# First group's tokens loaded first, normalized and turned ahead of the branch, and the folded output weights made in parts, in a three-stage attention and MLP kernel

## The chip, the cores and the metric

The kernel runs on one core of one Trainium2 chip. The metric is the device time of one execution in microseconds (us). The engines are named as in the profile: PE multiplies matrices, DVE, ACT and POOL work element by element, SP issues transfers (DMA). Each engine takes its instructions in order; between engines they wait on semaphores.

## The reference

The input `x` is (2, 256, 128, 128) in float32: B, T, FB and C. Three residual steps follow each other:

```python
cm = _causal_mask(x.shape[1])
bm = _band_mask(x.shape[2], BAND)                       # BAND = 16
xt = _ln(x, ln_t_w, ln_t_b).transpose(0, 2, 1, 3)
x = x + _mha(xt, t_wi, t_bi, t_wo, t_bo, H_T, cm).transpose(0, 2, 1, 3)
xf = _ln(x, ln_f_w, ln_f_b)
x = x + _mha(xf, f_wi, f_bi, f_wo, f_bo, H_F, bm)
xn = _ln(x, ln_n_w, ln_n_b)
h = jax.nn.gelu(xn @ w1.T + b1, approximate=False)
x = x + (h @ w2.T + b2)
```

`_ln` is a layer norm over C. `_mha` is attention with 4 heads of 32: three projections, scores with a mask, softmax, weighted sum, output projection. The first runs over T for each band with a causal mask, the second over the bands for each time with a band mask. The MLP is 128 to 512 to 128.

## The kernel before

**Two paths.** `load_constants` issues the loads of the weights (on ACT's queue) and of `cols`, `rows` and the first tokens `x0` (on SP's queue). `fold` (L341) multiplies the norm's scale into the projection weights (`wf`, `bq`) and bounds the scores from the weights: products `gk`, `gq`, `tests`, `tp`, then `ok`, `allok` and an integer `flag` on DVE. Every engine reads `flag` and branches (`tc.If`, L1161). With bounded scores `bounded_path` runs, in which softmax needs no maximum; this is the path of these inputs. The other one, `shifted_path`, is not executed.

**Groups.** The bounded path works on groups of 512 tokens (`NT` = 4 tiles of 128). A group is `OverTime` (attention over T), `OverBands` or `FeedForward`; there are 128 of each. A group's steps are methods:

- `statistics`: mean and variance on DVE (BATCH_NORM_STATS2, BATCH_NORM_AGGREGATE: `stats`, `mv`)
- `root_by_scalar`, `refine`: the inverse root by ln and exp on ACT (`lnv`, `root`), then three small operations on DVE (`vy`, `vy`, `rstd`)
- `normalize`: four operations on DVE that write `xh` with 33 elements to a row of 32
- `turn`: a transposition by 32x32 blocks on DVE (`z`) and four stores of `z` to a DRAM tile `turned`
- `fetch`: one load of `turned` as `xnT`, with the channels on the partitions
- `queries_keys`, `values`: the projections `qp`, `kp`, `vp` on PE, copied by ACT to `qT`, `kT`, `v`
- `time_scores`: the products `sp` of the new group's first half and the old group's second half, then exponentials `p` on ACT, masks and sums on POOL
- `weigh`, `invert`, `divide`, `output`, `finish`: `rp`, `op`, reciprocals, `u`, `oT`, `yp`, and the residual sum

**What `normalize` reads.** It takes its input through `longer`, which gives a slice of 160 elements, 32 more than a tile has:

```python
def longer(quad, i, a):
    return quad.rearrange("p s t c -> p (s t c)")[:, i * P - a : (i + 1) * P + D - a]
```

`a` is 0 for the first three tiles and 32 for the last. `x0` has the shape (P, NT, NT, C), and group g takes `x0[:, :, g]`.

**The order.** `run` (L1029) writes the order out by hand: for n from -12 on, it calls each step of the groups around n, and `InOrder` keeps each engine's instructions in that order. Normalizing group n+4 and fetching n+3 go ahead of the projections of n+2 and the scores of n and n+1. PSUM has 8 banks; `time_scores` takes them by name, and `bank` otherwise by turns. A tile that takes over a bank waits for the last reader of the one before.

**The folded rest.** At n = -4 `fold_rest` (L989) makes, for each attention, `bp` (a product of the value weights and the norm's shift), `bv`, the negated output weights `wn`, and `orow` (on ACT, multiplied by the output weights on PE as `op`, and summed with `rows` on DVE), then `b1p`, `b1` and `w1f` for the MLP. `warm` (L1022) follows with eight products of 384 columns whose result nobody reads.

Of the kernel before, what the change touches and what calls it, by code (L numbers as in the profile page):

```python
# [10 lines left out]
F32 = mybir.dt.float32  # L11
# [8 lines left out]
P = 128  # L20
# [3 lines left out]
EPS = 1e-5  # L24
# [14 lines left out]
def load_constants(ctx, tc, x, t_wiT, t_woT, f_wiT, f_woT, w1T, w2T, cols, rows):  # L39
    nc = tc.nc  # L40
    B, T, FB, C = x.shape
    k = Consts()
    k.NI = w1T.shape[1] // P
    const = ctx.enter_context(tc.tile_pool(name="const", bufs=1))
    k.const = const
    k.cols = const.tile([P, 16], F32, name="cols_sb")
    nc.sync.dma_start(k.cols, cols)
    k.rows = const.tile([P, 3, C], F32, name="rows_sb")
    for i in range(3):
        nc.sync.dma_start(k.rows[:, i, :], rows[i : i + 1, :].partition_broadcast(P).squeeze(1))  # L50


    k.x0 = const.tile([P, NT, NT, C], F32, name="x0")
    for i in range(NT):
        f = i // (T // P) * NT
        nc.sync.dma_start(k.x0[rows_of(i)], BoundedPath.of_times(x[0], i, slice(f, f + NT)))

    def weight(src, n, name):
        t = const.tile([P, n], F32, name=name)
        nc.scalar.dma_start(t, src)  # L60
        return t

    k.wiT = (weight(t_wiT, 3 * C, "t_wiT_sb"), weight(f_wiT, 3 * C, "f_wiT_sb"))
    k.woT = (weight(t_woT, C, "t_woT_sb"), weight(f_woT, C, "f_woT_sb"))
    k.w1T = weight(w1T, k.NI * P, "w1T_sb")
    k.w2T = const.tile([P, k.NI, C], F32, name="w2T_sb")
    nc.scalar.dma_start(k.w2T, w2T.rearrange("(j p) c -> p j c", p=P))
    k.ident = const.tile([P, P], F32, name="ident")
    make_identity(nc, k.ident)
    k.mhalf = const.tile([P, NT], F32, name="mhalf")  # L70
    nc.vector.memset(k.mhalf, -0.5)
    dram = ctx.enter_context(tc.tile_pool(name="dram", bufs=1, space=DRAM))
    k.x1 = [dram.tile([T, FB, C], F32, name=f"x1_{b}") for b in range(B)]
    return k
# [263 lines left out]
                    nc.sync.dma_start(outv[:, t0 + g : t0 + g + NT, :], res)  # L338


def fold(tc, k):  # L341

    nc = tc.nc
    const = k.const
    C = P
    scale = 1.0 / math.sqrt(D)
    tensor, vector, scalar = InOrder(tc, nc.tensor), InOrder(tc, nc.vector), InOrder(tc, nc.scalar)

    def col(i):
        return k.cols[:, i : i + 1]

    k.ones = const.tile([P, P], F32, name="ones")
    nc.vector.memset(k.ones, 1.0)
    k.wf, k.bq = [], []
    tests = const.tile([P, 6], F32, name="tests")
    with tc.tile_pool(name="foldp", bufs=2) as fp, tc.tile_pool(name="foldps", bufs=1, space=PSUM) as pp:
        scalar.preload_act_table_set(EXP_SET)

        bp = pp.tile([P, 2], F32, name="bp")
        for a in range(2):
            tensor.matmul(bp[:, a : a + 1], k.wiT[a][:, 0:C], col(5 * a + 1), start=True, stop=True)
        for a in range(2):
            c0 = 5 * a
            wf = const.tile([P, 3 * C], F32, name=f"wf{a}")
            vector.tensor_scalar(wf[:, 0:C], k.wiT[a][:, 0:C], col(c0), scale, ALU.mult, ALU.mult)
            vector.tensor_scalar(wf[:, C : 3 * C], k.wiT[a][:, C : 3 * C], col(c0), None, ALU.mult)
            bq = const.tile([P, 1], F32, name=f"bq{a}")
            vector.tensor_scalar(bq, bp[:, a : a + 1], col(c0 + 2), scale, ALU.add, ALU.mult)  # L370
            k.wf.append(wf)
            k.bq.append(bq)
        brs = []
        for a in range(2):
            brp = pp.tile([1, P], F32, name=f"brp{a}")
            tensor.matmul(brp, k.bq[a], k.ident, start=True, stop=True)
            br = fp.tile([1, P], F32, name="br")
            scalar.copy(br, brp)
            brs.append(br)

        for a in range(2):
            wf, wo = k.wf[a], k.woT[a]
            br = brs[a]
            gk = pp.tile([P, P], F32, name="gk", tag=f"gk{a}")
            tensor.matmul(gk, wf[:, C : 2 * C], wf[:, C : 2 * C], start=True, stop=True)
            gq = pp.tile([P, P], F32, name="gq", tag=f"gq{a}")
            tensor.matmul(gq, wf[:, 0:C], wf[:, 0:C], start=True, stop=False)
            tensor.matmul(gq, br, br, start=False, stop=True)
            gs = fp.tile([P, P], F32, name="gs")
            scalar.copy(gs, gk)  # L390
            vector.tensor_tensor(gs, gq, gs, ALU.mult)
            for h in range(H):
                r = rows_of(h)
                vector.tensor_reduce(tests[r, 3 * a : 3 * a + 1], gs[r, r], AX.X, ALU.add)
            for j, w in ((1, wf[:, 2 * C : 3 * C]), (2, wo)):
                sq = fp.tile([P, P], F32, name="sq")
                scalar.activation(sq, w, AF.Square, accum_out=tests[:, 3 * a + j : 3 * a + j + 1])
        tp = pp.tile([P, 6], F32, name="tp")
        tensor.matmul(tp, k.ones, tests, start=True, stop=True)
        ok = fp.tile([P, 6], F32, name="ok")  # L400
        for a in range(2):
            vector.tensor_scalar(
                ok[:, 3 * a : 3 * a + 1], tp[:, 3 * a : 3 * a + 1], SAFE * SAFE / (C * (C + 1)), None, ALU.is_le
            )
            vector.tensor_scalar(
                ok[:, 3 * a + 1 : 3 * a + 3], tp[:, 3 * a + 1 : 3 * a + 3], LARGE, None, ALU.is_le
            )
        allok = fp.tile([P, 1], F32, name="allok")
        vector.tensor_reduce(allok, ok, AX.X, ALU.min)
        flag = const.tile([P, 1], I32, name="flag")  # L410
        vector.tensor_copy(flag, allok)
    return nc.values_load(flag[0:1, 0:1], min_val=0, max_val=1)


# [10 lines left out]
class Group:  # L425
# [10 lines left out]
    def load(self):  # L436

        if self.before is not None:
            self.before()

    def bias(self):
        pass
# [196 lines left out]
def rows_of(h):  # L639
    return slice(h * D, (h + 1) * D)  # L640
# [223 lines left out]
class BoundedPath:  # L864
# [121 lines left out]
                for g, part, _, store in run:  # L986
                    yield FeedForward(self, partial(part, "x2", g), partial(part, "res", g), None, partial(store, g))

    def fold_rest(self):  # L989

        k, tensor, vector, scalar = self.k, self.tensor, self.vector, self.scalar
        C = P
# [1 line left out]
        def col(i):  # L994
            return k.cols[:, i : i + 1]

        k.wn, k.orow = [], []
        for a in range(2):
            c0 = 5 * a

            bp = self.bank([P, 1], "bp")
            tensor.matmul(bp, k.wiT[a][:, 2 * C : 3 * C], col(c0 + 1), start=True, stop=True)
            bv = self.small.tile([P, 1], F32, name="bv")
            scalar.activation(bv, bp, AF.Identity, bias=col(c0 + 4))
            wn = self.once.tile([P, C], F32, name=f"wn{a}")
            scalar.mul(wn, k.woT[a], -1.0)
            k.wn.append(wn)
            orow = self.once.tile([P, C], F32, name=f"orow{a}")
            scalar.activation(orow, k.ones, AF.Copy, scale=bv)
            op = self.bank([P, C], "op")  # L1010
            tensor.matmul(op, orow, k.woT[a], start=True, stop=True)
            vector.tensor_tensor(orow, op, k.rows[:, a, :], ALU.add)
            k.orow.append(orow)
        b1p = self.bank([P, k.NI], "b1p")
        for j in range(k.NI):
            tensor.matmul(b1p[:, j : j + 1], k.w1T[:, j * P : (j + 1) * P], col(11), start=True, stop=True)
# [2 lines left out]
        k.w1f = self.once.tile([P, k.NI * P], F32, name="w1f")  # L1019
        scalar.activation(k.w1f, k.w1T, AF.Copy, scale=col(10))  # L1020

    def warm(self):  # L1022


        for _ in range(8):
            bank = self.bank([P, 3 * P], "warm")
            self.tensor.matmul(bank, self.k.ones, self.k.wf[0], start=True, stop=True)

    def run(self, x, out):  # L1029
        groups = list(self.groups(x, out))  # L1030

        def do(n, *names):
            if 0 <= n < len(groups):
# [6 lines left out]
        def do_at(n, kind, *names):  # L1040
            if at(n, kind):
                do(n, *names)
# [4 lines left out]
        due = {n: [i for i in run0 if run0[0] + due[i] == n] for n in range(-12, len(groups) + 2)}  # L1047
        A = RUN // NT

        self.scalar.preload_act_table_set(EXP_SET)  # L1050
        for n in range(-12, len(groups) + 2):
            feeds = [at(n - 2 + i, FeedForward) for i in range(5)]
            bands = [at(n - 2 + i, OverBands) for i in range(5)]
# [36 lines left out]
            if n < 0:  # L1090
                do(n + 5, "statistics")
            do_at(n + 5, FeedForward, "statistics")
            if n == -4:
                self.fold_rest()
                self.warm()
            do(n - 1, "weigh")
            do(n - 1, "invert_exactly" if turn else "invert")
            if new is not None:
# [17 lines left out]
                    do_at(n + A, OverBands, "statistics", "root")  # L1116
            do_at(n + 2, OverTime, "queries_keys", "take_query", "take_key")
            do_at(n + 1, OverBands, "queries_keys", "take_query", "take_key")
            do_at(n + 5, OverTime, "root_by_scalar", "refine")
            for i in due[n]:  # L1120
                do(i, "root_by_scalar", "refine")
            do_at(n, OverTime, "bias")
# [1 line left out]
                do(n - 2, "output", "finish")  # L1124
            do_at(n + 2, OverTime, "values", "take_values")
            do_at(n + 1, OverBands, "values", "take_values")
            if old is not None or new is not None:

                b = self.banks
# [11 lines left out]
def conv_seq_kernel(  # L1141
# [15 lines left out]


    k = load_constants(ctx, tc, x, t_wiT, t_woT, f_wiT, f_woT, w1T, w2T, cols, rows)
    bounded = fold(tc, k)  # L1160
    with tc.If(bounded > 0) as cmp:  # L1161
        bounded_path(tc, k, x, out)
    with cmp.Else():
# [38 lines left out]
```

## Time and profile before

| what | value |
|---|---|
| time, median of 4 runs | 2710.82 us (2707.32 to 2711.22) |
| the profiled execution's own time | 2710.08 us |
| its span | 2708.4 us |
| mean granted clock of PE | 0.998 |
| busy: PE, DVE, ACT, POOL | 99%, 84%, 68%, 69% |
| `flag` written, first statistics | 12.84 us, 13.94 us |
| first `qp` | 27.39 us |

A row of the timeline has the start in us, the busy time in us, the engine, the line (L859 is the recording helper of all steps), the operation, output<-input, shapes and the count; in brackets the idle time before it and what ended it. SPq rows are transfers being issued, PEld rows are weight loads of PE. A row of busy time by stretches has the stretch, its length, then PE, PEld, DVE, ACT and POOL with the number of instructions, the granted clock, the DMA share and GB/s.

### The profile page before, as it was taken

How to read it: one execution, taken by the hardware profiler on the slowest of the kernel's cores; microseconds unless marked ns; L12 is line 12 of the kernel's file. 1: busy time of each engine (PE TensorE's matmuls, PEld its weight loads, DVE VectorE, ACT ScalarE, POOL GpSimd, SP SyncE). 2: the span in 40 equal slices, each digit the busy share in tenths (PEclk: the TensorE clock that was granted, in tenths of full speed). 3: DMA queues.
4: the chain of work that ended last, by engine and by line, in shares of the span. 5: the costliest groups of instructions: out<-in, count | busy, mean ns of one | idle time of the engine just before them, and what ended most of it. 6: DMA issues, size and time to landing. Idle time of an engine off the chain costs nothing.

```text
span 2708.4 us, 139654 instructions
## 1 busy us (share of the span) xinstructions
PE 2677.2 (99%) x60470; PEld 1832.1 (68%) x60470; DVE 2278.9 (84%) x6708; ACT 1845.0 (68%) x3620; POOL 1864.3 (69%) x2169
## 2 busy tenths in 40 slices
PE   8999999999999999999999999999999999999998
PEld 5676767666766666666667766666666666666665
DVE  7999999999999987868769779688697796886874
ACT  6888888888888874655745646557456465565563
POOL 4887888788878876667657666666676666665762
PEclk9999999999999999999999999999999999999999
DMA  6555555555555535445444444454444444544533
GB/s 155 140 150 143 149 150 142 148 151 143 149 144 148 143 100 131 108 120 133 109 124 125 111 127 115 118 130 114 121 126 110 124 119 118 130 110 123 134 92 84
DMA packets 471442, 346.00 MB, mean 128 GB/s; under 512 B 43296, under 2 KB 405152, under 8 KB 470816
## 3 DMA queue, kind: packets, MB, share of 16 engines
q1 hardware_dynamic: 469568, 335.92, 48.3%
q8 instruction: 476, 7.80, 1.3%
q14 instruction: 150, 1.23, 0.2%
q10 hardware_dynamic: 1248, 1.05, 0.2%
HBM read 169.03 MB, written 167.77 MB: 124 GB/s over the span
## 4 chain that ended last, share of the span: by engine, by line
PE 82%; DVE 14%; DMA 2%; issue 1%; ACT 0%; SPq 0%; DVEq 0%; ACTq 0%
PE zp L859 17%; PE hp L859 14%; PE sp L859 10%; PE op L859 8%; PE rp L859 7%; PE vp L859 7%; PE qp L859 6%; PE kp L859 6%; PE yp L859 6%; DVE xh L859 3%; DVE stats L859 2%; DVE z L859 2%; DVE u L859 2%; DVE rp L859 2%; DVE sp L859 1%; DVE x L859 1%
## 5 line engine op out<-in xcount | busy, mean ns | idle before, releaser
L859 ACT ACTIVATE hT<-hp,b 128x512 f32<-128x512 f32 x512 | 346.7, 687 | 533.1 <-PE hp L859 518.1
L859 POOL TENSOR_SCALAR_AFFINE_SELECT pf<-pf 128x512 f32<-128x512 f32 x768 | 477.0, 635 | 265.6 <-ACT pf L859 239.2
L859 DVE TENSOR_SCALAR xh<-x,mv,rstd 128x160 f32<-128x160 f32 x1536 | 596.7, 430 | 14.2
L859 PEld LDWEIGHTS zp<-w2T_sb,hT 128*32 128x32 f32 x16384 | 459.3, 110 | 61.5 <-issue 37.2
L859 PE MATMUL zp<-w2T_sb,hT 128*32 128x128 f32 x16384 | 475.7, 273 | 0.2 <-ACT hT L859 0.2
L859 PE MATMUL hp<-xnT,w1f 128*32 128x512 f32 x4096 | 474.6, 592 | 0.0
L859 ACT ACTIVATE p<-sp 128x512 f32<-128x512 f32 (+1 forms) x1024 | 417.1, 501 | 15.9 <-PE sp L859 4.2
L859 POOL TENSOR_SCALAR_AFFINE_SELECT p<-p 128x1024 f32<-128x1024 f32 x256 | 280.0, 1094 | 188.8 <-ACT p L859 188.8
L859 PE MATMUL sp<-qT,kT 32*128 32x128 f32 (+1 forms) x8192 | 361.4, 310 | 3.2 <-DVE oT L859 1.8
L859 PEld LDWEIGHTS sp<-qT,kT 32*128 32x128 f32 x8192 | 309.4, 185 | 56.8 <-ACT kT L859 47.9
L859 PEld LDWEIGHTS vp<-wf,xnT 128*32 128x32 f32 x8192 | 232.8, 110 | 157.2 <-issue 138.8
L859 POOL TENSOR_TENSOR p<-p,p 128x512 f32<-128x512 f32 x256 | 328.7, 1284 | 10.7
L859 DVE BATCH_NORM_STATS2 stats<-x 128x6 f32<-128x128 f32 x1536 | 326.9, 275 | 0.1
L859 ACT ACTIVATE pf<-sp 128x512 f32<-128x512 f32 x512 | 264.7, 603 | 60.4 <-PE sp L859 59.6
L859 PEld LDWEIGHTS hp<-xnT,w1f 128*32 128x32 f32 x4096 | 156.3, 110 | 189.9 <-issue 115.5
L859 DVE STREAM_TRANSPOSE z<-xh 128x512 f32<-128x512 f32 x384 | 273.2, 712 | 13.2
L859 DVE TENSOR_TENSOR res<-zp,res 128x512 f32<-128x512 f32 x128 | 87.4, 683 | 223.7 <-PE zp L859 223.2
L859 PE MATMUL yp<-wn,oT 128*32 128x128 f32 x8192 | 272.1, 273 | 0.0
L859 PE MATMUL vp<-wf,xnT 128*32 128x128 f32 x8192 | 270.9, 273 | 0.0
L859 POOL TENSOR_TENSOR rstd<-rstd,mhalf 128x4 f32<-128x4 f32 x248 | 256.6, 1035 | 20.7
L859 PE MATMUL qp<-xnT,wf 128*32 128x512 f32 x2048 | 267.3, 592 | 2.0 <-ACT p L859 2.0
L859 ACT ACTIVATE qT<-qp,bq 128x512 f32<-128x512 f32 x256 | 176.0, 688 | 134.4 <-PE qp L859 134.2
(92 smaller groups left out, 4001.6 us busy)
## 6 DMA issues: line engine op xcount, KB each, us to landing
turned<-z SPq DMA_DIRECT2D x1536, 64.0 KB, 2.3
xnT<-turned SPq DMA_DIRECT2D x384, 256.0 KB, 3.1
x<-in_x SPq DMA_DIRECT2D x128, 256.0 KB, 4.2
x<-res SPq DMA_DIRECT2D x256, 128.0 KB, 2.4
x<-x SPq DMA_DIRECT2D x128, 256.0 KB, 4.3
out<-res SPq DMA_DIRECT2D x256, 128.0 KB, 2.5
w1T_sb<-in_w1T ACTq DMA_DIRECT2D x1, 256.0 KB, 6.0
w2T_sb<-in_w2T ACTq DMA_DIRECT2D x1, 256.0 KB, 7.6
```

The costliest lines, as they stand in the source:

```text
L859: return self.tc.keep_in_program_order(emit(*args, **kwargs))
```

## The change

The first tokens are loaded in two portions: token 0 of each block of `x0` in four loads of 64 KB, then `rows`, then the remaining three tokens in four loads of 192 KB. Group 0's `statistics`, `root_by_scalar`, `refine`, `normalize`, `turn` and `fetch` and group 1's `statistics`, `root_by_scalar` and `refine` are issued inside `fold`, ahead of the branch, in tiles of their own; in the bounded path these steps are emptied by `follow`. `warm` becomes twelve products of 128 columns inside `fold`, behind `tp`. `fold_rest` is made in three parts: part 0 behind `values` of group 0, part 1 behind those of group 1, part 2 behind those of group 2. For n < 0, `root_by_scalar` and `refine` of group n+5 come behind `values`. The second load of the activation table is gone.

```diff
+    def tokens(a, n):
+        for i in range(NT):
+            f = i // (T // P) * NT + a
+            nc.sync.dma_start(k.x0[rows_of(i), :, a : a + n], BoundedPath.of_times(x[0], i, slice(f, f + n)))
+
+    tokens(0, 1)
     k.rows = const.tile([P, 3, C], F32, name="rows_sb")
     for i in range(3):
         nc.sync.dma_start(k.rows[:, i, :], rows[i : i + 1, :].partition_broadcast(P).squeeze(1))
-    for i in range(NT):
-        f = i // (T // P) * NT
-        nc.sync.dma_start(k.x0[rows_of(i)], BoundedPath.of_times(x[0], i, slice(f, f + NT)))
+    tokens(1, NT - 1)
...
+class Ahead:
+    def __init__(self, ctx, tc, k):
+        self.tc, self.k = tc, k
+        self.vector, self.scalar, self.sync = InOrder(tc, tc.nc.vector), InOrder(tc, tc.nc.scalar), InOrder(tc, tc.nc.sync)
+        self.pool = ctx.enter_context(tc.tile_pool(name="ahead", bufs=1))
+        self.work = self.small = self
+        self.dram = ctx.enter_context(tc.tile_pool(name="aheadd", bufs=1, space=DRAM))
...
+    def group(self, g):
+        def src(i=None, a=0):
+            return self.k.x0[:, :, g] if i is None else BoundedPath.longer(self.k.x0, i * NT + g, a)
+
+        return OverTime(self, src, None)
...
-def fold(tc, k):
+def fold(ctx, tc, k):
...
+    ahead = Ahead(ctx, tc, k)
+    k.first = g0, g1 = ahead.group(0), ahead.group(1)
...
             k.bq.append(bq)
+        g0.statistics()
+        g0.root_by_scalar()
+        g0.refine()
         brs = []
...
             brs.append(br)
+        g0.normalize()
+        g0.turn()
...
         tensor.matmul(tp, k.ones, tests, start=True, stop=True)
+
+        warm = pp.tile([P, P], F32, name="warm", tag="gk0")
+        for _ in range(12):
+            tensor.matmul(warm, k.ones, k.wf[0][:, 0:C], start=True, stop=True)
+        g1.statistics()
+        g1.root_by_scalar()
+        g0.fetch()
         ok = fp.tile([P, 6], F32, name="ok")
...
         vector.tensor_copy(flag, allok)
+        g1.refine()
     return nc.values_load(flag[0:1, 0:1], min_val=0, max_val=1)
...
+    def follow(self, ahead):
+        done = ["statistics", "root_by_scalar", "refine"]
+        self.mv, self.rstd = ahead.mv, ahead.rstd
+        if hasattr(ahead, "xnT"):
+            self.xnT = ahead.xnT
+            done += ["normalize", "turn", "fetch"]
+        for name in done:
+            setattr(self, name, lambda: None)
...
-    def fold_rest(self):
+    def fold_rest(self, part):
...
-        k.wn, k.orow = [], []
-        for a in range(2):
+        if part == 0:
+            k.wn, k.orow = [], []
+        if part < 2:
+            a = part
...
             k.orow.append(orow)
+            return
         b1p = self.bank([P, k.NI], "b1p")
...
-    def warm(self):
-        for _ in range(8):
-            bank = self.bank([P, 3 * P], "warm")
-            self.tensor.matmul(bank, self.k.ones, self.k.wf[0], start=True, stop=True)
-
     def run(self, x, out):
         groups = list(self.groups(x, out))
+        for g, ahead in zip(groups, self.k.first):
+            g.follow(ahead)
...
-        self.scalar.preload_act_table_set(EXP_SET)
         for n in range(-12, len(groups) + 2):
...
             if n < 0:
                 do(n + 5, "statistics")
             do_at(n + 5, FeedForward, "statistics")
-            if n == -4:
-                self.fold_rest()
-                self.warm()
...
-            do_at(n + 5, OverTime, "root_by_scalar", "refine")
+            if n >= 0:
+                do_at(n + 5, OverTime, "root_by_scalar", "refine")
...
             do_at(n + 2, OverTime, "values", "take_values")
             do_at(n + 1, OverBands, "values", "take_values")
+            if n < 0:
+                if n >= -2:
+                    self.fold_rest(n + 2)
+                do(n + 5, "root_by_scalar", "refine")
+            if n == 0:
+                self.fold_rest(2)
```

## The prediction

> **What bounds the kernel now.** I read the page first, then busy time by stretches, the timeline of the first 60 us and the DMA answers there.
>
> ```profile
> span 2708.4 us, 139654 instructions
> PE 2677.2 (99%) x60470; PEld 1832.1 (68%) x60470; DVE 2278.9 (84%) x6708; ACT 1845.0 (68%) x3620; POOL 1864.3 (69%) x2169
> ```
> ```profile
> 27.40:48.86 21.46, 18.26 (x333) 10.73 (x332) 17.69 (x61) 18.54 (x44) 11.59 (x11) 1.00 0.55 151
> 48.86:2650.00 2601.14, 2591.28 (x58864) 1773.79 (x58868) 2226.04 (x6526) 1800.35 (x3524) 1840.11 (x2141) 1.00 0.50 128
> ```
>
> PE is the bound from 48.86 us on (2591.28 of 2601.14 busy; a round of the first branch takes 7.30 us and PE is busy for all of it). Behind that point the built program of the changed kernel has the same instructions in the same order on each engine. So the change is worth what it moves the moment at which PE stops waiting, and that moment lies in these rows of the timeline:
>
> ```profile
> 3.34 3.39 SPq L56 DMA_DIRECT2D x<-in_x  x4
> 13.78 0.06 DVE L881 MEMSET eps<- 128x1 f32 x1 [0.79 <-DVE flag L859]
> 18.73 1.78 SPq L859 DMA_DIRECT2D turned<-z  x4
> 20.42 7.04 PE L859 MATMUL warm<-wf,ones 128*128 128x384 f32 x16
> 21.70 1.61 DVE L859 TENSOR_SCALAR xh<-x,mv,rstd 128x160 f32<-128x160 f32 x4
> 22.00 0.34 SPq L859 DMA_DIRECT2D xnT<-turned  x1
> 27.39 1.06 PE L859 MATMUL qp<-xnT,wf 128*32 128x512 f32 x8
> 32.42 1.07 PE L859 MATMUL qp<-xnT,wf 128*32 128x512 f32 x8 [1.16 <-ACT p L859]
> 40.67 1.04 DVE L859 SCALAR_TENSOR_TENSOR vy<-mv,root 128x4 f32<-128x4 f32 x1 [1.34 <-ACT root L859]
> 41.74 1.21 DVE L859 SCALAR_TENSOR_TENSOR vy<-vy,root 128x4 f32<-128x4 f32 x1
> 48.86 1.51 PE L859 MATMUL sp<-qT,kT 32*128 32x256 f32 x20 [0.69 <-DVE u L859]
> ```
>
> The first projection (qp, 27.39) waited for the warming products, not for its xnT (issued at 22.00, about 3.0 us to landing). The second waited for ACT's exponentials. 21.70 is where DVE starts to normalize the second group.
>
> **The trap in the first part.** The last loads of the first tokens land late: the four x<-in_x are issued at 3.34 to 6.3 us, and the DMA answer for the last gives
>
> ```profile
> x<-in_x SPq DMA_DIRECT2D x1, 256.0 KB, 7.4
> ```
>
> 6.3 + 7.4 = 13.7 us. From 3.5 to 13.7 us the DMA engines move 184 GB/s on average and are never idle: this is the whole initial load, and the change only reorders it. Statistics of group 0 read token 0 alone and need the four small loads. But `normalize` reads through `longer` (L915), 160 elements where the token has 128: 32 of the next token (of the previous one for the last block). In the built program the first xh of group 0 therefore waits for all four remaining loads, and the last of these is issued only after w1T has landed (3.53 + 6.0 = 9.5 us). xh cannot start before about 13.7 us, and behind it on DVE stand z, gs, tests and the flag of the branch. Bounds for that moment: 10 us (9.5 and hardly any transfer) to 16 us (shorter pieces, 1.5 KB in place of 2 KB, and the lanes' waits). I take 13.7, where the same bytes end now.
>
> **The sum, from 13.7.** On DVE: xh and z 2.35 (16.35 to 18.70), 16.05. gs and tests twice, 1.07 each (8.56 to 9.63), 18.2. Statistics of group 1, 1.02 (18.63 to 19.65), 19.3; tp lies beside them (0.74 from tests to ok). ok, allok and flag 0.76 (12.25 to 13.01), 20.0. Refining group 1, 0.6, 20.6. Flag read and branch 0.77 (13.01 to 13.78), of which some 0.1 overlaps: xh of group 1 starts at about 21.3, against 21.70. What was gained by four steps done early is eaten by the flag that comes 7 us later; 0.4 us is left.
>
> From there DVE does z (23.6), statistics of group 2 (24.7), ln and root on ACT 0.63, refine 0.65, xh and z 2.36 (28.3), statistics of group 3 (29.3): these rows have the old lengths.
>
> On PE: tp after tests, then 24 passes of the twelve warming products from 18.8. A pass of 128 columns takes 0.213 there (b1p, 8 passes between 18.85 and 20.42, the same step for gq at 7.09 to 7.30), so 5.1, 23.9; branch 0.77: qp of group 0 at 24.7. Its xnT is there by 22.4 (z at 16.05, 3.3 to the issue as from 18.70 to 22.00, 3.0 to land). So qp starts 2.7 earlier than 27.39. qp, kp, vp 2.66 (27.46 to 30.12), 27.4; then the first part of the folded weights: v copied 0.7 behind, bv, wn, orow 0.76 (17.46 to 18.22), 28.8; op 0.80 (18.27 to 19.06), 29.6. The score products sp stand behind op on PE, and the third of them needs op's bank, which DVE frees with orow behind statistics of group 3 (29.3 + 0.24 = 29.6). Both paths meet at 29.6. First exponentials 0.8 later, 30.4; two of them 1.07; qp of group 1 at 31.5, against 32.42.
>
> Its xnT is just there: SP now issues four loads of x (1 MB) right behind the branch, all in front of the second turned, where before there were two (22.38). 512 KB took 2.5 us of packets (14.8 to 17.3), so 1 MB holds the queue from 22 to 27; turned goes out behind it, xnT is issued at about 28.2 (now 28.38) and lands at 31.2. That leaves 0.3 us of slack.
>
> Group 1 has its own part of the weights between vp and sp: 4.5 from qp to sp (2.66, 0.7, 0.76, op 0.45 at the faster step) where the row now has 2.73 (32.42 to 35.15). Loss 1.8: sp at 36.05 against 35.15, qp of group 2 at 38.55 against 37.63.
>
> Group 2 gets b1p, 8 passes, 0.86 at the faster step, and one more wait. Two of the last sp products use b1p's bank, freed by b1 on DVE, and b1 stands behind refine of group 5. That refine is the slow one: 40.67 to 44.19, each small operation ending with a POOL operation (1.04, 1.21, 1.20). Shifted by 0.9 it starts at 41.55 and frees b1 between 44.1 and 45.2. Queued on PE behind the two products are rp, op and qp of group 3. I take 44.1: sp ends 44.35, rp and op 2.3, qp 46.7 (now 44.74), the three projections 2.65, twelve sp 0.74: 50.1 where PE now resumes at 48.86. **+1.3 us.**
>
> The queues that steps are moved past: SP now waits for turned to land (19.4) before it reads the flag (20.0), ACT does ln and root of group 1 (19.9) before it does, both with little to spare; POOL gets nothing new. The rest costs nothing on the path: ACT's second table load (1.28 at 13.64) goes, but ACT waited for mv until 15.19; rows_sb moves behind small loads and is read at 29, not 19.7; w1f (0.71) lies between v and sp; the two waits of orow on DVE are counted above; eps0 and the names that `follow` empties issue nothing in time.
>
> **The clock.** Warming products were 0.64 us apart until 23.12 and 0.32 from 23.75 on, after PE had worked without a gap since 18.26 (5.5 us): PE ran at half its step till then.
>
> The changed kernel has 5.1 us of gapless warming, then a gap of 0.8 at the branch. If the faster step comes before 24, the sum stands. If it comes during the first projections, at 27.5 to 30 us, these take up to twice 2.66: +2.6 to +3.8 in place of +1.3.
>
> [...]
>
> **Rivals.** (a) It does what it says: xh doesn't wait, because the remaining tokens come much earlier than 13.7. For it: only 256 KB are asked first, and the queue has bubbles (about 90 GB/s between 5 and 6 us). Against it: the wait stands in the program and the bytes are the same. At 10 us the chain above gives -2.4; with no wait at all DVE would reach xh at about 8.5, where the last bq and gs stand now, and the sum is -3.9. Even that is inside 0.2%.
>
> (b) Slower: the clock stays at the half step through group 1. Place: the projections, op and sp of groups 0 and 1, about 6.5 us of PE work per group that would take 13. PE would have gaps there (1.2 us before each qp, over 1 us before each op). Price: +4.1 if the rise comes at 32 us, +5.4 at 36, +8.1 at 45. It decides from about 36 us on.
>
> (c) The second xnT comes late, behind 1 MB of x: each us over the slack of 0.3 delays the end by one; two loads more than before are 2.5 us of packets, so at most +2.2 on top.
>
> **How the numbers follow.** The profiled execution took 2710.08 us (span 2708.4 and 1.7 around it), 0.74 under the median of the runs, 2710.82. 2710.08 + 1.3 = 2711.4, and on the scale of the median 2712.1. About 0.2% (5.4 us) is what a measurement of this kernel can tell from no change. Chances: the forecast, with the clock rising in the warming or in the first projections, 0.67; (a) 0.13, half-way to being visible only if the weights' parts also cost less than counted; (b) 0.12; (c) 0.08. The range runs from (a)'s end, 2710.8 - 3.9 = 2706.9, to the forecast with late clock and xh at 16 us, +4.5, and some of (b): 2717. Faster 0.07, same 0.77, slower 0.16.
>
> **What would show it.** Right: xh of group 0 idle until a DMA lands at 12.8 to 14.5 us; xh of group 1 at 21 to 22; qp at 24 to 25.5, 31 to 33 and 38 to 40; PE waiting for orow ahead of two sp blocks, and for b1 ahead of the third; PE gapless from about 50 to 52. Wrong: xh of group 0 at 9 us, or qp of group 1 before 29, or a round after 60 us that isn't 7.30.

## The result, and the profile after

The changed kernel takes 2715.32 us (median of 32 runs, 2713.35 to 2717.87), the kernel before 2710.68 us (median of 52 runs made beside it, 2706.97 to 2712.6). The ratio is 1.0019, with a 95% interval of 1.0014 to 1.0024: slower by 4.6 us. That is just inside the 0.2% that the prediction called no change (the interval reaches beyond it), and inside its range. The profiled execution took 2713.69 us.

The page's first lines, against those of the kernel before:

```profile
span 2711.9 us, 139676 instructions
PE 2676.6 (99%) x60478; PEld 1830.9 (68%) x60478; DVE 2279.3 (84%) x6709; ACT 1844.2 (68%) x3619; POOL 1866.5 (69%) x2169
```

PE's busy time is the same (2676.6 against 2677.2), the span is 3.5 us longer: PE waits more. Busy time by stretches shows where; the first row goes from group 1's first projection (qp) to group 2's, the second from group 3's on. After the bounds come the length, busy time and instructions of PE, PEld, DVE, ACT and POOL, the granted clock, the DMA share and GB/s.

```profile
31.78:41.27 9.49, 7.58 (x84) 4.37 (x84) 4.13 (x24) 4.93 (x14) 1.09 (x1) 0.74 0.62 163
...
50.78:2650.00 2599.22, 2589.15 (x58836) 1770.00 (x58832) 2224.63 (x6518) 1803.41 (x3531) 1844.06 (x2140) 1.00 0.53 128
```

Behind 50.78 us PE is busy as before. In group 1's stretch the mean clock is 0.74. PE's rows of the timeline:

```profile
18.21 5.27 PE L913 MATMUL warm<-wf,ones 128*128 128x128 f32 x24
23.54 1.07 PE L913 MATMUL qp<-xnT,wf 128*32 128x512 f32 x8
...
27.69 0.49 PE L913 MATMUL op<-t_woT_sb,orow 128*128 128x128 f32 x2 [1.04 <-ACT orow L913]
...
29.29 1.46 PE L913 MATMUL sp<-qT,kT 32*128 32x256 f32 x12 [0.48 <-DVE orow L913]
31.78 1.93 PE L913 MATMUL qp<-xnT,wf 128*32 128x512 f32 x8 [1.03 <-DMA xnT<-turned]
33.46 1.96 PE L913 MATMUL kp<-xnT,wf 128*32 128x512 f32 x8
35.16 1.86 PE L913 MATMUL vp<-wf,xnT 128*32 128x128 f32 x32
...
41.27 1.06 PE L913 MATMUL qp<-xnT,wf 128*32 128x512 f32 x8 [0.87 <-ACT p L913]
...
44.81 1.05 PE L913 MATMUL b1p<-cols_sb,w1T_sb 128*128 128x1 f32 x8 [0.74 <-ACT v L913]
...
47.95 0.71 PE L913 MATMUL sp<-qT,kT 32*128 32x128 f32 x6 [0.57 <-DVE b L913]
```

The projections of group 1 (31.78 to 36.95) take 1.93, 1.96 and 1.86 us, where those of groups 0 and 2 take 1.04 to 1.07: the clock had risen at 23.14, near the end of the warming (18.21 to 23.48), and was back at a half from 29.96 to 36.79. Busy time of PE in the stretches of 3.41 us in which the clock's records change, with the granted clock behind it:

```profile
26.55:29.96 3.41, 1.88 (x17) 1.00 0.24 66
29.96:33.37 3.41, 2.38 (x16) 0.50 0.82 227
33.37:36.79 3.42, 3.42 (x44) 0.50 0.64 176
```

Before the fall PE worked for 1.88 us of 3.41, between the waits ahead of op and of the third sp product. It came up again behind a stretch that was busy throughout.

The rows of DVE's timeline answer to those of before: group 0's xh waits for the remaining tokens, group 1's xh stands at 21.03 (21.70 before), and b1 (`b`) leaves DVE at 47.75 behind the slow refine of group 5.

```profile
13.22 1.61 DVE L913 TENSOR_SCALAR xh<-x,mv,rstd 128x160 f32<-128x160 f32 x4 [4.85 <-DMA x<-in_x]
...
21.03 1.61 DVE L913 TENSOR_SCALAR xh<-x,mv,rstd 128x160 f32<-128x160 f32 x4
...
44.32 1.04 DVE L913 SCALAR_TENSOR_TENSOR vy<-mv,root 128x4 f32<-128x4 f32 x1 [1.35 <-ACT root L913]
...
47.75 0.15 DVE L913 TENSOR_TENSOR b<-b1p,cols_sb 128x4 f32<-128x4 f32 x1
```

From the starts of qp the balance can be drawn up (us; before: 27.39, 32.42, 37.63, 44.74, 67.94 for groups 0, 1, 2, 3 and 6; after: 23.54, 31.78, 41.27, 50.78, 72.81). The rows not shown so far, of the kernel before, then of the changed one:

```profile
37.63 1.06 PE L859 MATMUL qp<-xnT,wf 128*32 128x512 f32 x8 [0.89 <-ACT p L859]
44.74 1.04 PE L859 MATMUL qp<-xnT,wf 128*32 128x512 f32 x8
...
67.94 1.04 PE L859 MATMUL qp<-xnT,wf 128*32 128x512 f32 x8
```
```profile
50.78 1.04 PE L913 MATMUL qp<-xnT,wf 128*32 128x512 f32 x8
...
72.81 1.04 PE L913 MATMUL qp<-xnT,wf 128*32 128x512 f32 x8
```

| stretch | before | after | difference | forecast |
|---|---|---|---|---|
| start to qp of group 0 | 27.39 | 23.54 | -3.85 | -2.7 |
| group 0 to 1 | 5.03 | 8.24 | +3.21 | +1.8 |
| group 1 to 2 | 5.21 | 9.49 | +4.28 | +1.8 |
| group 2 to 3 | 7.11 | 9.51 | +2.40 | +1.0 |
| group 3 to 6 | 23.20 | 22.03 | -1.17 | -0.7 |
| sum | | | +4.87 | +1.2 (stated as +1.3) |

From there the distance stays until 960 us. The two profiled executions end only 3.6 us apart, because the clock also falls once in each where the first branch ends, for 6.83 us in the kernel before (962.4 to 969.2) and for 3.41 us in the changed one (968.6 to 972.0).

### The profile page after: what moved, and what is told of

Its sections match the earlier page's. It is cut to its first block, busy times and chain, and to the rows that moved or that the text cites. A ratio compares the mean times of both kernels' runs of the same rounds, so it can differ in the third digit from the quotient of the medians.

```text
span 2711.9 us, 139676 instructions
## 1 busy us (share of the span) xinstructions
PE 2676.6 (99%) x60478; PEld 1830.9 (68%) x60478; DVE 2279.3 (84%) x6709; ACT 1844.2 (68%) x3619; POOL 1866.5 (69%) x2169
## 3 DMA queue, kind: packets, MB, share of 16 engines
q10 hardware_dynamic: 1248, 1.05, 0.1%
## 4 chain that ended last, share of the span: by engine, by line
PE 82%; DVE 13%; DMA 3%; issue 1%; SPq 0%; ACT 0%; DVEq 0%
PE zp L913 17%; PE hp L913 14%; PE sp L913 10%; PE op L913 8%; PE rp L913 7%; PE vp L913 7%; PE qp L913 6%; PE kp L913 6%; PE yp L913 6%; DVE xh L913 3%; DMA xnT<-turned 2%; DVE z L913 2%; DVE stats L913 2%; DVE u L913 2%; DVE rp L913 1%; DVE x L913 1%
## 5 line engine op out<-in xcount | busy, mean ns | idle before, releaser
L913 DVE STREAM_TRANSPOSE z<-xh 128x512 f32<-128x512 f32 x384 | 273.3, 712 | 13.7
L913 PE MATMUL kp<-xnT,wf 128*32 128x512 f32 x2048 | 268.0, 594 | 0.0
```

The costliest lines, as they stand in the source:

```text
L913: return self.tc.keep_in_program_order(emit(*args, **kwargs))
```

## The experiments

Theory: the second half of the change, the weights' parts between projections and scores, costs PE its waits, and these make the clock fall in group 1; the fall is worth about 2.5 us. Rivals: the chain over DVE and POOL to b1 sets the end whatever the clock is; the early loads of later tokens (1 MB in front of the second `turned`) set it; or the trap in `normalize` does. Each profile is one execution. "Group 6" is the start of its qp against 67.94 in the kernel before.

| kernel | group 6 | median, us | ratio to before, 95% interval |
|---|---|---|---|
| the change | +4.9 | 2715.32 | 1.0014 to 1.0024 |
| e1_no_spill | 0.0 | 2712.52 | 0.9997 to 1.0015 |
| e2_fill | +2.8 | 2714.13 | 1.0006 to 1.0024 |
| e3_two_loads | +3.8 | 2714.31 | 1.0008 to 1.0026 |
| e4_parts_in_fold | +4.1 | 2712.04 | 1.0000 to 1.0018 |
| e6_fold_loads | +0.1 | 2712.27 | 0.9992 to 1.0010 |
| e7_parts_alone | +6.3 | 2716.42 | 1.0012 to 1.0031 |
| e8_no_spill_fill | -1.8 | 2710.28 | 0.9989 to 1.0007 |
| e5_best | -4.2 | 2707.17 | 0.9975 to 0.9993 |
| e9_later_loads | +4.9 | 2717.80 | 1.0016 to 1.0037 |
| e10_before_bridge | +0.3 | 2710.86 | 0.9994 to 1.0012 |
| e11_later_loads_bridge | +6.5 | 2718.11 | 1.0017 to 1.0036 |
| e12_best_bridge | -3.4 | 2706.12 | 0.9974 to 0.9992 |

**Work in PE's waits.**

```diff
+            for _ in range(5):
+                tensor.matmul(op, k.ones, k.woT[a], start=True, stop=True)
             tensor.matmul(op, orow, k.woT[a], start=True, stop=True)
...
+            if n == -1:
+                spare = self.bank([P, P], "spare", self.banks["b0"])
+                for _ in range(5):
+                    self.tensor.matmul(spare, k.ones, k.wf[0][:, 0:P], start=True, stop=True)
             do_at(n + 2, OverTime, "queries_keys", "take_query", "take_key")
```

> The changed kernel with products that nobody reads put where PE waits: five of 128 columns into op's bank ahead of each op product, five into a spare bank between the first score block and the projections of group 1. They use time in which PE had nothing to do. Theory (the clock fell back at 29.96 because PE had been waiting, and the 6.83 us at half cost 2.65 us): the clock stays at 1.0 from about 23 us on, the projections of group 1 take 2.7 us in place of 5.3, qp of group 2 is at 38.5 to 39 in place of 41.27, and the gapless rounds start 2.2 to 2.6 us earlier than in the changed kernel: time 2712.6 to 2713.1. Rival (the chain over DVE and POOL to b1 sets the end whatever PE's clock is): qp of group 2 moves, but qp of group 3 stays near 50.8 and the time near 2715.3. A third possibility: the clock falls at the same moment in spite of the fillers, and nothing moves.

Rows of PE's timeline in this kernel, and the stretches of its clock:

```profile
30.40 1.38 PE L913 MATMUL spare<-wf,ones 128*128 128x128 f32 x10
32.20 1.06 PE L913 MATMUL qp<-xnT,wf 128*32 128x512 f32 x8 [0.41 <-ACT p L913]
...
39.24 1.07 PE L913 MATMUL qp<-xnT,wf 128*32 128x512 f32 x8 [0.88 <-ACT p L913]
```
```profile
26.78:30.19 3.41, 3.02 (x29) 1.00 0.32 62
30.19:33.60 3.41, 3.00 (x30) 1.00 0.78 223
```

No fall. Group 1 takes 7.04 us (32.20 to 39.24) in place of 9.49, so the fall cost 2.45 us, and the parts by themselves 7.04 - 5.21 = 1.83. From there the whole chain moves: group 3's qp is at 48.73 (50.78 in the changed kernel), so b1 was not what held the end. Group 6 gains 2.05. The medians differ by 1.2 us and the intervals overlap, so what is shown is shown by the trace. The mean clock of each run, which is on record, agrees with it: averaged over the runs it is 0.9969 in the changed kernel, 0.9983 in e2_fill and 0.9988 in the kernel before beside it. So the fall is not a chance of the one traced execution.

**Two loads in place of four.**

```diff
-            for i in (2 * n + 12, 2 * n + 13) if n < -2 else (n + 10,) if n < 2 else ():
+            for i in (2 * n + 12, 2 * n + 13) if n < -3 else (2 * n + 10, 2 * n + 11) if -3 < n < 0 else (n + 10,) if 0 <= n < 2 else ():
```

> The changed kernel with two loads of tokens in place of four in front of the second group's transposed tiles; the two others come two turns later. Theory (1 MB in front of turned makes xnT of group 1 late): qp of group 1 no longer waits for a DMA but for ACT's exponentials, and starts 0.4 to 0.7 us earlier, at 31.1 to 31.4 in place of 31.78; that alone gives 2714.6 to 2714.9. If the shorter wait also keeps the clock up, the gain is 3 us (2712.3). Rival: other transfers take the place of the loads and nothing moves, 2715.3.

A miss: qp of group 1 now waits for the exponentials, as expected, but starts at 31.62, 0.16 earlier instead of 0.4 to 0.7. The clock blurs this comparison. A row of ACT in the changed kernel, then one of ACT and one of PE in this one:

```profile
30.05 2.07 ACT L913 ACTIVATE p<-sp 128x512 f32<-128x512 f32 x4 [0.42 <-PE sp L913]
```
```profile
30.48 2.06 ACT L913 ACTIVATE p<-sp 128x512 f32<-128x512 f32 x4 [0.95 <-PE sp L913]
...
31.62 1.94 PE L913 MATMUL qp<-xnT,wf 128*32 128x512 f32 x8 [0.35 <-ACT p L913]
```

Here the clock fell 2.0 us earlier (27.96 against 29.96), the score products of group 0 ran at a half, and the exponentials began 0.43 later. qp started 1.14 behind them; from 30.05 in the changed kernel that would be 31.19. So an estimate from these rows is that the 1 MB cost 0.6 us there; it was not measured apart from the clock. The other 0.9 us of group 6's gain comes from the clock: it fell at 27.96 and rose at 34.79, so that less of group 1's projections lay in the half (8.61 us from group 1 to 2).

**The parts ahead of the branch.** bv, wn, orow, op and b1p, b1, w1f move into `fold`, and none of them stands behind the projections. This leaves the change's first half. The second kernel has the two loads as well.

```diff
+        for a in range(2):
+            tensor.matmul(bp[:, 2 + a : 3 + a], k.wiT[a][:, 2 * C : 3 * C], col(5 * a + 1), start=True, stop=True)
...
+            tensor.matmul(op, orow, k.woT[a], start=True, stop=True)
+            vector.tensor_tensor(orow, op, k.rows[:, a, :], ALU.add)
+            k.orow.append(orow)
         g0.normalize()
...
-                if n >= -2:
-                    self.fold_rest(n + 2)
...
-            if n == 0:
-                self.fold_rest(2)
```

> The changed kernel with the folded output weights (bv, wn, orow, op, b1p, b1, w1f) made ahead of the branch, while DVE waits there for the remaining tokens, and none of it behind the projections. It is the change's first half alone, in effect. Theory (the parts cost 1.8 us in group 1 and 1.2 us at b1, and bring the gaps that let the clock fall): sp of group 0 follows its projections without a wait for orow, qp of group 1 at 31 to 31.4, its projections take 2.7 us, qp of group 2 at 36.5 to 37.5, and the first gapless round starts 1 us later to 2 us earlier than in the kernel before: 2709 to 2711.5. Rival (the clock falls in any case once PE has waited for xnT): group 1's projections still take 5 us, and the time is 2712 to 2713.5.

> The kernel of e4_parts_in_fold with two loads of tokens in place of four in front of the second group's transposed tiles. There PE stood still for 5.82 us until xnT of group 1 landed at 34.16 us, behind 1 MB of tokens. Theory (that megabyte, not the folded weights, is what e4 paid): xnT of group 1 lands 1 to 3 us earlier, qp of group 1 at 31.2 to 33; the clock still falls (PE waits for over 2.5 us in one stretch), and the first gapless round comes 1.5 to 3 us later than in the kernel before: 2711 to 2712. Rival (DVE's normalizing and the way through DRAM set that moment): qp of group 1 stays within 0.4 us of 34.16 and the time at 2712.

One row of PE's timeline from each, first with four loads, then with two:

```profile
34.16 1.93 PE L934 MATMUL qp<-xnT,wf 128*32 128x512 f32 x8 [5.82 <-DMA xnT<-turned]
```
```profile
30.62 1.94 PE L934 MATMUL qp<-xnT,wf 128*32 128x512 f32 x8 [2.73 <-ACT p L934]
```

With four loads the second xnT is the bound (rival (c) of the prediction). This was a miss: qp of group 1 was expected at 31 to 31.4 with its projections at full speed, and the rival, that the clock falls in any case, was right. With two loads qp of group 1 starts 3.5 us earlier, and earlier than the 31.2 to 33 expected; group 6 is level with the kernel before (+0.1), where 1.5 to 3 us later was expected. The clock falls in both (31.57 and 30.61 us), behind stretches in which PE stood idle for 2.7 us or more in one piece. The second xnT came 2.4 us later in e4_parts_in_fold than in the changed kernel, with the same four loads in front of it. Those loads were issued 1.26 us later (21.80 against 20.54), which is about half of it; the rest is open. Groups 2 to 3 take 7.13 in both, 7.11 in the kernel before: without the parts the 2.4 us there are gone.

**The second half alone**, on the kernel before. The parts stand behind the projections; the warming has sixteen products in place of eight, as nothing stands in front of it.

```diff
-                self.fold_rest()
...
-        for _ in range(8):
+        for _ in range(16):
...
+            if -2 <= n <= 0:
+                self.fold_rest(n + 2)
```

> The kernel before with the second half of the change alone: the folded output weights in three parts behind the first projections, group 0 after the branch as before; the warming has sixteen products in place of eight, since the parts no longer stand ahead of it. Theory (the parts cost PE 1.8 us in group 1 and 1.2 us at b1, and their gaps let the clock fall): qp of group 0 at 26 to 28, the second block of scores and qp of group 2 1.5 to 2.5 us later than in the kernel before if the clock stays up, 3.5 to 5 if it falls; the gapless rounds 2 to 3 us later (2712.7 to 2713.7), or 4 to 5 with a fall (2714.7 to 2715.7). Rival (the parts are harmless by themselves, and the loss comes from the early group 0): the gapless rounds start within 0.7 us of the kernel before.

Rows of PE's timeline:

```profile
33.93 1.94 PE L859 MATMUL qp<-xnT,wf 128*32 128x512 f32 x8 [0.77 <-ACT p L859]
...
39.81 0.49 PE L859 MATMUL op<-f_woT_sb,orow 128*128 128x128 f32 x2 [1.08 <-ACT orow L859]
...
49.39 0.71 PE L859 MATMUL sp<-qT,kT 32*128 32x128 f32 x6 [0.57 <-DVE b L859]
```

The same waits and the same kind of fall (33.97 to 37.38), and 6.3 us at group 6 where 4 to 5 were expected: from qp of group 0 (26.39) to that of group 1 it lost 2.5 us as well, 7.54 against 5.03, which I had not counted. This half alone is as slow as the whole change (ratio 1.0022 against 1.0019); the rival, that the parts are harmless by themselves, is out.

**Without the trap.** Group 0's `normalize` reads the 128 elements of its own token.

```diff
-        return OverTime(self, src, None)
+        return (Exact if g == 0 else OverTime)(self, src, None)
...
+class Exact(OverTime):
...
+                xh[:, i * run : i * run + H * row].rearrange("p (c w) -> p c w", w=row)[:, :, 0:D], self.src()[:, i, :],
```

> The changed kernel, except that normalize of group 0 reads exactly the 128 elements of its own token (group 0 only). So xh of group 0 no longer needs the remaining loads; the first instruction that does is now the statistics of group 1, which still stands ahead of the flag. Theory (the remaining loads, not the branch, hold the first group): xh of group 0 at 8.4 to 8.6 us in place of 13.22, flag at about 15 in place of 19.30, xh of group 1 at 16.3 to 17 in place of 21.03, qp of group 0 at 18.5 to 19.5 in place of 23.54; if the rest follows, the first gapless round starts 4 to 4.7 us earlier than in the changed kernel and the time is 2710.6 to 2711.3, that is level with the kernel before. Rival (the loads of later tokens or the clock set the pace behind the branch): qp of group 0 is early, but half or more of the 4.5 us is gone by qp of group 3, and the time is 2713 to 2715.

DVE's timeline in this kernel:

```profile
8.75 1.12 DVE L926 TENSOR_SCALAR xh<-x,mv,rstd 128x128 f32<-128x128 f32 x4
...
13.02 0.88 DVE L926 BATCH_NORM_STATS2 stats<-x 128x6 f32<-128x128 f32 x4 [0.34 <-issue]
...
16.37 1.61 DVE L926 TENSOR_SCALAR xh<-x,mv,rstd 128x160 f32<-128x160 f32 x4
```

The read across the token's edge cost 4.66 us for group 1's xh (21.03 to 16.37) and 4.9 us at group 6, all of it kept: the rival with the later loads is out. The median gained only 2.8 us, less than expected (2712.52 against 2710.6 to 2711.3), and the runs spread from 2707.62 to 2714.51; the profiled one was the 2707.62, in which the clock didn't fall where the first branch ends. It did fall from 23.88 to 30.71. The next kernel adds the products of e2_fill:

> e1_no_spill and e2_fill together: group 0 reads its own 128 elements, and products that nobody reads stand where PE waits for orow and ahead of the projections of group 1. In e1 the clock was at a half from 23.88 to 30.71 us. Theory (gaps ahead of op and qp bring the fall): no fall there, qp of group 1 at 27.5 to 28.3, its projections 2.7 us, the gapless rounds 2 to 2.6 us earlier than in e1, that is 2 to 2.6 us earlier than in the kernel before: median 2709 to 2710, and the spread of the runs smaller than e1's 7 us. Rival (the fall's moment is set by something else than PE's gaps): a stretch at a half remains before 40 us and the median stays near 2712.5.

The stretches of the clock in e1_no_spill, then the one at the same place here:

```profile
20.46:23.88 3.42, 1.81 (x24) 1.00 0.69 144
23.88:27.29 3.41, 2.07 (x12) 0.50 0.31 114
```
```profile
22.16:25.58 3.42, 2.90 (x28) 1.00 0.22 58
```

No half stretch is left before 40 us, and over all runs the mean clock went from 0.9966 to 0.9981. Group 6 is at -1.8, where -2 to -2.6 was expected; qp of group 0 was 1.0 later than in e1_no_spill (19.02; its warming took 5.38 us against 4.74). The median of 2710.28 just misses the 2709 to 2710 expected. The spread stayed at 6.2 us, a miss: in this profile the clock falls at 960.82.

**All together.** e5_best joins three edits from above (exact read; parts in `fold`, here behind the tests of the scores instead of ahead of group 0's `normalize`; two loads) and ten products ahead of the projections of group 1.

> Attempt at a version better than both: group 0 reads its own 128 elements, the folded output weights are made ahead of the branch, two loads of tokens in place of four stand in front of the second transposed tiles, and ten products that nobody reads keep PE busy ahead of the projections of group 1. Theory (all three costs are separate and add up): qp of group 0 at 18 to 19.5, qp of group 1 at 26.5 to 28, group 2 5.2 us later, no fall of the clock before 40 us, and the gapless rounds 4 to 5.5 us earlier than in the kernel before: median 2705 to 2707, 0.998 to 0.9985 of it. Rival (the loads of later tokens then arrive too late): qp of group 3 or 4 waits for a DMA, and less than half of that is left.

Two rows of PE's timeline:

```profile
27.77 1.06 PE L947 MATMUL qp<-xnT,wf 128*32 128x512 f32 x8 [1.29 <-DMA xnT<-turned]
...
33.86 1.07 PE L947 MATMUL qp<-xnT,wf 128*32 128x512 f32 x8 [1.77 <-DMA xnT<-turned]
```

Group 6 stands at -4.2, as expected, though qp of group 0 came later (20.18), and the median of 2707.17 (2705 to 2707 expected) is 4.4 us under the 2711.61 of the kernel before beside it: ratio 0.9984 (0.9975 to 0.9993). The interval excludes no change, but the gain is under 0.2%. The clock does not fall before 958.64. What is left are waits for xnT, and I tried to take them by loading one group of tokens per step:

```diff
-            for i in (2 * n + 12, 2 * n + 13) if n < -3 else (2 * n + 10, 2 * n + 11) if -3 < n < 0 else (n + 10,) if 0 <= n < 2 else ():
+            for i in (n + 8,) if n < 4 else ():
```

> The kernel of e5_best with one load of tokens in front of each of the first transposed tiles in place of two. There the projections of groups 1, 2 and 3 waited 1.29, 1.77 and 0.80 us for xnT. Theory (those waits are the loads standing in front): groups 1 and 2 no longer wait more than 0.5 us for a DMA, the gapless rounds start 1 to 2.5 us earlier than in e5_best, 5 to 6.5 earlier than in the kernel before, median 2704.7 to 2706.2. Rival (DVE's normalizing sets xnT, or a later load is then missed): the waits stay or move to statistics of a later group, and the median is within 0.7 us of e5_best's 2707.2.

A miss: the median is 10.6 us over e5_best's, more than theory or rival allowed. The rival was right in kind, a later load is missed. qp of group 1 came at 27.03 with no wait for a DMA, but DVE's statistics then waited 3.55 us for a DMA until 32.54, ACT's exponentials stood behind them, and qp of group 2 came at 35.83 after a wait of 4.48 us (33.86 in e5_best). The larger loss, 6.4 us, lies between groups 5 and 6, where statistics found no tokens (a row of DVE, then one of PE):

```profile
61.81 0.87 DVE L947 BATCH_NORM_STATS2 stats<-x 128x6 f32<-128x128 f32 x4 [5.63 <-DMA x<-in_x]
```
```profile
65.93 0.72 PE L947 MATMUL sp<-qT,kT 32*128 32x256 f32 x10 [3.53 <-DVE res L947]
```

**The fall at the end of the first branch.** Six products in the gap of 1.83 us there, in the kernel before and in the two above:

```diff
+        if new is None and (h, second, s) == (0, 0, 0):
+            path = old.path
+            spare = path.bank([P, P], "spare", path.banks["a0"])
+            for _ in range(6):
+                path.tensor.matmul(spare, path.k.ones, path.k.wf[0][:, 0:P], start=True, stop=True)
```

> The kernel before, with six products that nobody reads put into the 1.83 us in which PE waits at 961.3 us, where the first branch ends; nothing else. In the kernel before the granted clock was 0.5 from 962.4 to 969.2 us and the products there took twice as long. Theory (a gap of about 1 us or more in a stretch of 3.41 us makes the clock fall, and the fall costs about half of its length): no stretch at a half in the middle of the span, the second branch starts 2.5 to 3.4 us earlier, the median is 2707.5 to 2709, and the runs at 2711 to 2713 become rare. Rival (the fall comes from the change of the kind of work, or from a limit on power, and not from the gap): the stretch at a half stays and the time is that of the kernel before, within 0.7 us.

> e9_later_loads with the six products of e10_before_bridge at the end of the first branch. Theory: both gains add, median 2702.5 to 2704.5, about 0.997 of the kernel before. Rival (the clock falls there anyway): the median of e9_later_loads.

> e5_best with the same six products at the end of the first branch. Theory: 2 to 3 us less than e5_best, 2704 to 2705.2. Rival: e5_best's 2707.2 again.

All three missed what was expected: 2710.86 us against 2707.5 to 2709, 2718.11 against 2702.5 to 2704.5, and 2706.12 against 2704 to 2705.2. The row of PE's timeline in e10_before_bridge shows why this tells nothing of the cause:

```profile
962.80 2.90 PE L864 MATMUL spare<-wf,ones 128*128 128x128 f32 x12 [1.11 <-DVE u L864]
```

The bank I took was not free until DVE had written u; the products came when the clock had already fallen (962.78) and cost 2.90 us at a half. The stretch became 3.42 us in place of 6.83, and the second branch stands no more than 0.15 us ahead of the kernel before (qp at 1010.75 against 1010.90), 0.4 us better than at group 6. e12_best_bridge has 2706.12 us, 0.9983 of the kernel before; that it is better than e5_best is not shown.

## Why the prediction was right, and where it was off

That the time stays within 0.2% was right, and so was the trap: group 0's xh waited for the remaining tokens until 13.22 (13.7 forecast), and group 1's xh started at 21.03 (21.3). qp of group 0 came at 23.54, 1.2 earlier than the 24.7 forecast: the tokens landed 0.5 earlier, and the 0.77 us I had put down for the branch did not show between the warming (ends 23.48) and qp. qp of group 1 at 31.78 (31.5) and the round of 7.28 (qp of groups 5 and 6 at 65.53 and 72.81) fit too.

Part of this is luck. The early qp of group 0 was lost again by group 1, as sp waited for DVE's orow until 29.29 and qp for xnT until 31.78, the two paths that the sum had. The loss of 4.87 us is four times the +1.2 that the sum's own terms give (50.1 - 48.86 is 1.24), and it stayed inside 0.2% by a little. Of the signs named, qp of group 0 (23.54, not 24 to 25.5) and qp of group 2 (41.27, not 38 to 40) lay outside. Two readings were off without weight: b1p's rows give 0.196 us a pass, not 0.213 (the 24 passes took 5.27 us, 5.1 forecast), and the DMA engines were busy for 0.85 of 3.5 to 13.7 us, not without a pause.

The term that was mis-sized is **the clock**. The sum took it that a rise inside the warming lets the rest run at full speed. The clock did rise there (23.14), and fell back at 29.96, for 2.45 us in group 1. The prediction had a price for a half-speed group 1, in rival (b), +5.4 us with the rise at 36 us; that is nearer to the measured 4.87 than the forecast's 1.3. But it looked for a late rise, where the trace shows a fall after a rise (29.96 after 23.14), behind the thin stretch that the change's own waits make (1.04 ahead of op, 0.48 ahead of sp). The sum counted these gaps as lost time; rival (b) saw them only as what delays the rise. The parts themselves were sized well: 1.8 forecast in group 1, 1.83 measured with the clock up.

The second mis-sized term is **b1**: from qp of group 2 to that of group 3 the forecast had +1.0, measured +2.40, of which 1.17 were given back later (forecast 0.7). I took the lower end of 44.1 to 45.2 for b1, that is 5.55 after qp of group 2; it was 6.48 after (47.75 - 41.27), near the upper end, as each of the three operations of the slow refine took its full 1.04 to 1.21 us. b1p waited 0.74 for ACT's v and took 1.05 where I had counted 0.86 for the product alone, but that did not set the end: sp waited for b 0.57 us longer.

Of rival (c), the megabyte in front of the second turned: PE's wait at 31.78 did end with xnT, but taking half of the megabyte away gave 0.16 us there, some 0.6 by the estimate above. It becomes the bound as soon as the parts don't stand in front (5.82 us in e4_parts_in_fold). Rival (a), no wait, didn't come true; made true by the exact read it was worth 4.9 us at group 6, from +4.9 to 0.0; the prediction had 5.2 between the two cases, from +1.3 to -3.9.

The clock's records of the changed kernel change at 23.14, 29.96, 36.79, 968.63 and 972.04 us: 6.83, 6.83, 931.84 and 3.41 us apart, that is 2, 2, 273 and 1 times 3.413. The rise came 4.9 us after the start of the warming (18.21), in the kernel before 5.5 us after the end of PE's last gap (18.27 to 23.73). The fall at 29.96 came behind a stretch in which PE worked for 1.88 of 3.41 us and waited for no more than 1.04 us in one piece.

## What to carry to other kernels

Work that was moved off the start into PE's stream cost twice here, as PE waited for another engine's share of it: the parts by themselves 1.83 us in group 1, and the fall of the clock from 29.96 to 36.79 another 2.45 us. Where such waits can't be avoided, try to cover them: in e2_fill products with weights of 128*128 kept the clock at 1.00 there and gained 2.05 us at group 6. Or keep the small product chains together ahead of the dense part: with two loads, that brought group 6 from +3.8 (e3_two_loads) to +0.1 (e6_fold_loads). And before an early start is counted on, look at what its first instruction reads: here 32 elements of the neighbouring token cost the early start 4.7 us.

## What the runs showed of the hardware

PE's busy time alone doesn't decide the fall. Rows of the kernel before, then one of e5_best, in the same columns as above:

```profile
30.55:33.97 3.42, 2.26 (x32) 1.00 0.59 157
...
958.99:962.40 3.41, 2.31 (x52) 1.00 0.44 122
```
```profile
30.22:33.63 3.41, 1.87 (x47) 1.00 0.46 142
```

The first and the last (2.26 and 1.87 us busy) were not followed by a fall, the second (2.31 us) was, at 962.40. Nor does the length of a wait alone, as the expectation of e10_before_bridge had it (a gap of about 1 us or more): in the first PE waited for 1.16 us ahead of qp at 32.42, in the last for 1.54 of the 1.77 us ahead of qp at 33.86.

Another difference is how large the weights are that the products use; the largest here have 128*128 elements. An estimate from the rows of PE's timeline: let each pass count its columns times the share of 128*128 that its weights fill, so that a pass of warm or of op with orow (128*128, 128 columns) counts 128, a pass of sp (32*128, 256 columns) 64. The three stretches above then come to 2454, 1488 and 1828. The stretch ahead of the fall in the changed kernel (26.55 to 29.96) comes to 1039: two passes of op, 256, and some twelve of sp, 782. The one in its place in e2_fill (26.78 to 30.19) comes to some 2400, as the ten passes ahead of op add 1280. Cut into stretches of 3.41 us that lie as the clock's changes do, from the stretch ahead of the first rise on, the traces of the kernel before and of the changed one have 1573. The six that one at a half followed count 468 to 1488; the 1567 that one at full speed followed count 1595 (43.62 to 47.03 in the changed kernel) or more. This was counted afterwards, on two executions: no kernel was run to test it, and that the clock goes by this count is not shown.

The runs of one kernel differ by nearly 7 us (e1_no_spill) without a change of program, and where the stretches of 3.41 us lie against the kernel's start differs from profile to profile: the first rise came at 23.73 us in the kernel before, 23.14 in the changed one, 21.13 in e3_two_loads. So the same wait falls differently into the stretches. At the wait of 1.83 us where the first branch ends the lowest stretch counts 1488 in the kernel before and 468 in the changed one, and the clock fell in both; in e1_no_spill, e4_parts_in_fold and e6_fold_loads it did not fall there. These three end 2.2 to 2.5 us better against the kernel before than they stood at group 6. The clock of every run points the same way: of the 29 runs of the kernel before made beside e10_before_bridge, the six with a mean clock of 1.000 took 2707.32 to 2708.45 us, the nine with 0.998 took 2710.43 to 2712.33. That this makes the spread is likely, but only one execution of each kernel was traced.
